# Two SBUF pools for the operands of a cross-attention, and a padded row for its last key block

## The chip, the cores and the metric

The kernel runs on one core of one Trainium2 chip, in one launch. The metric is the device time of that core in microseconds. The host only lays the inputs out; all arithmetic is on the core. Engines are named as the profile names them: PE is TensorE's matmul, PEld its weight load, DVE is VectorE, ACT is ScalarE, POOL is GpSimd, SP issues the DMAs.

## The reference, cut to what matters

The model is two perceiver layers on 8 sequences of 64 tokens with 512 features, and a context of 8 x 1601 rows of 512 features. The change touches the first attention alone:

```python
x = x + L0_xattn(layernorm(x), ctx, Wq, bq, Wkv, bkv, Wo, bo)   # touched
x = x + L0_attn(layernorm(x), ...)      # a state-space scan
x = x + L0_ffn(layernorm(x), ...)       # ternary weights
x = x + L1_xattn(layernorm(x), ctx)     # one head, no projections
x = x + L1_attn(layernorm(x), ...)
x = x + L1_ffn(layernorm(x), ...)

def L0_xattn(query, kv, ...):           # 32 heads, 8 groups of keys, head size 128
    q = (query @ Wq + bq)               # 8 groups x 4 heads
    k, v = split(kv @ Wkv + bkv)        # 1601 keys for each of 8 sequences
    scores = einsum(q, k) / sqrt(128)
    o = einsum(softmax(scores), v)
    return o @ Wo + bo
```

## The kernel before, in words

The first attention is walked by `x_all` as 64 units: 8 sequences, and in each 8 key groups `i`. A unit has the 4 x 64 = 256 queries of one group and goes over the 1601 keys in six blocks (`BLK`): five of 256 keys and a last one of 322, of which 1601 are real keys in all. Both float32 operands of a projection are split in a high and a low part, each of type fp32r, and a product is the sum of three matmuls, (0,0), (0,1) and (1,0). Over the four chunks of 128 features that is 12 matmuls into one PSUM tile. The steps, each with the names that the profile shows:

- `x_ctx` (blocks `cxb`, last block `cxt`): loads a block of the transposed context chunk by chunk into `cst`, and splits it: ACT copies the high part, POOL subtracts for the low part (lines 101 and 102). A block is made once for a sequence and used by all 8 groups.
- `x_k` (line 354, PSUM tile `k_ps`): the keys. The stationary operand is the weight tile `wk`, the moving one is `cxb` with 256 columns or `cxt` with 322. ACT and DVE split the result into `kt` (lines 104, 105).
- `x_v` (line 325, `v_ps`): the values of 128 keys for two groups at once. The stationary operand is 128 columns of `cxb` or `cxt`, the moving one is the weight tile `wv` with 256 columns. ACT copies the result into `v`.
- `x_s` (line 374, `s_ps`): the scores. Stationary `kt`, moving `q`, three matmuls for 128 keys. ACT copies them into `S` (line 377), DVE keeps a running maximum in `mx` (line 381).
- `x_max`, `x_spread`, `x_exp`: of the unit before, the maximum is made one per query, spread over the partitions, subtracted (DVE, line 415) and exponentiated (ACT, line 416); POOL sums into `ss` (lines 418, 426).
- `x_av` (line 438, `o_ps`): stationary `v`, moving `S`, in plain float32.
- `x_o` and `x_wo` (line 495, `w_ps`): normalisation into `ot`, and for each pair of sequences the product with the output weights, stationary `ot`, moving `wo` with 512 columns.

Beside this stream runs side work: `prep` (weights of the later layers are split and stored) and, for each finished pair of sequences, `chain` (all later layers for that pair). The recording order interleaves the two by planned shares, and the engines execute in that order. The last pair's chain stands alone at the end, from about 2400 us on; for it the pools of the first attention are closed and the pool `tp` takes their place.

Tiles come from pools, and a pool's place in SBUF follows from the order in which pools are opened. Before, one pool `xp` holds all tiles of the first attention. The pools `const`, `xw` and `xp` lie from the bottom up; `qp` and later `cp` lie at the top. In the built kernel the tiles stand so (KB from the start of a partition):

| tile | before | after |
|---|---|---|
| `cxb` (5 buffers) | 55.25 to 95.25 | 19.25 to 59.25 |
| `q` | 114.69 to 118.69 | 59.25 to 63.25 |
| `v` (16) | 120.69 to 136.69 | 63.25 to 79.25 |
| `cxt` | 136.69 to 146.75 | 79.25 to 89.75 |
| `ot` | 150.81 to 154.81 | 89.75 to 93.75 |
| `S` (12) | 23.25 to 47.25 | 93.75 to 117.75 |
| `wk` (2) | 47.25 to 55.25 | 117.75 to 125.75 |
| `cst` (3) | 95.25 to 99.09 | 125.75 to 129.69 |
| `kt` (3) | 99.09 to 106.69 | 129.69 to 137.56 |
| `wv` | 106.69 to 114.69 | 137.56 to 145.56 |
| `wo` (3) | 154.81 to 166.81 | 151.62 to 163.62 |

Of the kernel before, what the change touches and what calls it, by code (L numbers as in the profile page):

```python
# [9 lines left out]
FR = mybir.dt.float32r  # L10
# [6 lines left out]
P = 128  # L17
D = 512
NC = 4
T = 64  # L20
LK = 1601
LP = 1602
NKV = 8
G = 4
NT = 13
# [13 lines left out]
VB, SB = 16, 12  # L39
# [36 lines left out]
class Kernel:  # L76
# [214 lines left out]
    def x_ctx(self, b, k):  # L291

        nc = self.nc
        o, w = BLK[k]
        if k == 5:
            t = self.sb("cxt", [P, 2, NC, 322], FR, pool=self.xp, bufs=1)
        else:
            t = self.sb("cxb", [P, 2, NC, 256], FR, pool=self.xp, bufs=5)
        for c in range(NC):
            st = self.sb("cst", [P, 322], pool=self.xp, bufs=3)  # L300
            nc.sync.dma_start(out=st[:, :w], in_=self.i["ctxT"][b, c, :, o : o + w])
            self.split(t[:, 0, c, :], t[:, 1, c, :], st[:, :w], eng=nc.gpsimd)
        self.ctxb[(b, k)] = t
# [6 lines left out]
    def x_v(self, b, j, t):  # L310

        nc = self.nc
        if j not in self.wv_t:
            w = self.sb("wv", [P, 2, NC, 256], FR, pool=self.xp, bufs=1)
            nc.sync.dma_start(out=w.bitcast(FP), in_=self.wv_s[j])
            self.wv_t = {j: w}
        w = self.wv_t[j]
        ps = self.px.tile([P, D], FP, name=self.nm("v_ps"), tag="kv", bufs=KVB)[:, :256]
        blk, o = (5, 256) if t == 12 else (t // 2, (t % 2) * P)
        r = rows_of(t)  # L320
        cx = self.cblk(b, blk)
        k = 0
        for c in range(NC):
            for a, m in ((0, 0), (0, 1), (1, 0)):
                nc.tensor.matmul(ps[:r], lhsT=cx[:, a, c, o : o + r], rhs=w[:, m, c, :], start=k == 0, stop=k == 11)  # L325
                k += 1
        vt = self.sb("v", [P, 256], pool=self.xp, bufs=VB)
        nc.scalar.copy(vt[:r], ps[:r])  # L328
        self.v[(b, j, t)] = vt

# [7 lines left out]
        self.wkt[(b, i)] = w  # L338

    def x_q(self, b, i):  # L340
        q = self.sb("q", [P, 2, 256], FR, pool=self.xp, bufs=2)
        self.nc.sync.dma_start(out=q.bitcast(FP), in_=self.q_s[i][b].rearrange("p l g t -> p l (g t)"))
        self.q[(b, i)] = q

    def x_k(self, b, i, blk, w):

        nc = self.nc
        wd = BLK[blk][1]
        cx = self.cblk(b, blk)
        ps = self.px.tile([P, D], FP, name=self.nm("k_ps"), tag="kv", bufs=KVB)  # L350
        k = 0
        for c in range(NC):
            for a, m in ((0, 0), (0, 1), (1, 0)):
                nc.tensor.matmul(ps[:, :wd], lhsT=w[:, a, c, :], rhs=cx[:, m, c, :], start=k == 0, stop=k == 11)  # L354
                k += 1
        kt = self.sb("kt", [P, 2, 322], FR, pool=self.xp, bufs=3)
        self.split(kt[:, 0, :wd], kt[:, 1, :wd], ps[:, :wd], bias=self.bk[:, i : i + 1])
        return kt

# [80 lines left out]
    def x_o(self, b, i):  # L440

        nc = self.nc
        ps = self.o.pop((b, i))
        self.S.pop((b, i))
        r = self.l.pop((b, i))
        nc.tensor.matmul(ps[:, 1], lhsT=self.ones, rhs=r, start=True, stop=True)
        w = self.sb("rw", [P, 256], pool=self.xp, bufs=1)
        nc.scalar.activation(r, ps[:, 1], AF.Ln)
        nc.scalar.activation(r, r, AF.Exp, scale=-1.0)
        nc.vector.tensor_tensor(w, ps[:, 1], r, ALU.mult)  # L450
        nc.vector.scalar_tensor_tensor(r, w, 2.0, r, ALU.subtract, ALU.mult, reverse0=True)
        oa = w
        nc.vector.tensor_tensor(oa, ps[:, 0], r, ALU.mult)

        odd = b % 2
        oav = oa.rearrange("p (g t) -> p g t", t=T)
        scr = self.ot_s[b // 2][i]
        if b < 2:
            ot = self.sb("ot", [P, 1, G, 2, T], pool=self.xp, bufs=OTB)
            nc.scalar.activation(ot[:, 0, :, odd], oav, AF.Identity, bias=self.bv[:, i : i + 1])  # L460
        else:
            ot = self.sb("ot", [P, 2, G, 2, T], FR, pool=self.xp, bufs=OTB)
            self.split(ot[:, 0, :, odd], ot[:, 1, :, odd], oav, bias=self.bv[:, i : i + 1])
        if odd:
            nc.sync.dma_start(out=ot[:, :, :, 0].bitcast(FP), in_=scr)
            self.ot[(b, i)] = ot
        else:
            nc.sync.dma_start(out=scr, in_=ot[:, :, :, 0].bitcast(FP))
# [507 lines left out]
    def xattn1(self, bs, x, xo):  # L976
# [7 lines left out]
        def scores(k, b):  # L984
            q0 = k * T
            if self.tail:
                s = self.sb("bc", [T, LP])
                S = [s[:, :512], s[:, 512:1024], s[:, 1024:]]
# [252 lines left out]
    def run(self):  # L1241
        nc, tc, ctx = self.nc, self.tc, self.ctx
        nc.scalar.preload_act_table_set("natural_log_exp_and_others")
        self.setup(bufs=BUFS, accb=2, hs=4, tail=False, ahead=1, **TAGS)
        self.pc = ctx.enter_context(tc.tile_pool(name="pc", bufs=2, space=PSUM))
        xctx = ctx.enter_context(ExitStack())
        self.px = xctx.enter_context(tc.tile_pool(name="px", bufs=2, space=PSUM))
        self.consts()
        self.scratch()
        self.xw = ctx.enter_context(tc.tile_pool(name="xw", bufs=2))  # L1250
        self.xp = xctx.enter_context(tc.tile_pool(name="xp", bufs=2))
        qctx = ctx.enter_context(ExitStack())
        self.q_ln(qctx.enter_context(tc.tile_pool(name="qp", bufs=2, side="right")))
        B = self.B
        sizes = GROUPS.get(B) or [1] * B
        groups, k = [], 0
        for m in sizes:
            groups.append(list(range(k, k + m)))
            k += m
        self.place = {b: (k * T, len(g) * T) for g in groups for k, b in enumerate(g)}  # L1260
        side, self.tp = [], None

        def start(gen, now, cost, end):
            env = {k: getattr(self, k) for k in ENV}
            if not self.tail:
                env["nc"] = Side(self, PINNED)
            side.append({"gen": gen, "cost": cost, "got": 0.0, "t0": now, "end": end, "env": env})

        def advance(now):
            base = {k: getattr(self, k, None) for k in ENV}  # L1270
            for c in list(side):
                self.setup(**c["env"])
                goal = c["cost"] * min(1.0, (now - c["t0"]) / max(c["end"] - c["t0"], 1e-9))
                if now >= c["end"]:
                    goal = 1e9
                while c["got"] < goal:
                    try:
                        c["got"] += next(c["gen"])
                    except StopIteration:
                        if PRINT_COST:  # L1280
                            print("side", c["got"])
                        side.remove(c)
                        break
            self.setup(**base)

        gi, now, xdone = 0, 0.0, 0.0
        for cost, fin in self.x_all(list(range(B))):
            xdone += cost
            advance(xdone / X_COST)
            if fin == 0:  # L1290
                qctx.close()
                self.cp = ctx.enter_context(tc.tile_pool(name="cp", bufs=2, side="right"))
                start(self.prep(), xdone / X_COST, PREP_COST, PREP_END)
            if fin is not None and gi < len(groups) and groups[gi][-1] == fin:
                g = groups[gi]
                now = xdone / X_COST
                last = gi == len(groups) - 1
                if last:
                    self.pinning = False
                    xctx.close()  # L1300
                    self.pc = ctx.enter_context(tc.tile_pool(name="pt", bufs=3, space=PSUM))
                    self.cp = self.tp = ctx.enter_context(tc.tile_pool(name="tp", bufs=2))
                    self.setup(bufs=BUFS_TAIL, accb=6, hs=8, tail=True, ahead=2, **TAGS_TAIL)
                start(self.chain(gi, g), now, CHAIN_COST, now + SPAN[gi])
                if last:
                    side.insert(0, side.pop())
                gi += 1
        while side:
            now += 0.01
            advance(now)  # L1310
# [10 lines left out]
OTB = 1  # L1321
# [35 lines left out]
def _layout(inp):  # L1357
# [7 lines left out]
    r["ctxN"] = cx  # L1365
    ct = np.zeros((B, D, LP), f)
    ct[:, :, :LK] = np.transpose(cx, (0, 2, 1))
# [68 lines left out]
```

## Time and profile before

| | us |
|---|---|
| median of 3 runs | 2748.9 |
| lowest and highest | 2741.76, 2750.92 |
| the profiled execution | 2747.45 |
| its span, first to last instruction | 2745.6 |
| PE busy in it | 2584.6 |
| stretch from 60 to 2400 us: PE busy | 2281.36 of 2340.00 |
| stretch from 2400 us to the end: PE busy | 260.00 of 345.60 |

The profile is of one execution, whose time lies between the lowest and the highest of the runs. Matmul records overlap: each reaches from the issue to the modelled end of its last column, so a record is longer than the distance to the next one. The distance from start to start tells how fast PE goes through a group.

### The profile page before, as it was taken

How to read it: one execution, taken by the hardware profiler on the slowest of the kernel's cores; microseconds unless marked ns; L12 is line 12 of the kernel's file. 1: busy time of each engine (PE TensorE's matmuls, PEld its weight loads, DVE VectorE, ACT ScalarE, POOL GpSimd, SP SyncE). 2: the span in 40 equal slices, each digit the busy share in tenths (PEclk: the TensorE clock that was granted, in tenths of full speed). 3: DMA queues.
4: the chain of work that ended last, by engine and by line, in shares of the span. 5: the costliest groups of instructions: out<-in, count | busy, mean ns of one | idle time of the engine just before them, and what ended most of it. 6: DMA issues, size and time to landing. Idle time of an engine off the chain costs nothing.

```text
span 2745.6 us, 47783 instructions
## 1 busy us (share of the span) xinstructions
PE 2584.6 (94%) x17840; PEld 2303.7 (84%) x17840; DVE 1756.7 (64%) x2988; ACT 1378.4 (50%) x3318; POOL 1163.1 (42%) x1175
## 2 busy tenths in 40 slices
PE   7999999999999899999999989999999999976778
PEld 6999999889889899978988988988897998954545
DVE  4544345577777886545587787454668787549645
ACT  4444555444556554544456555444556555435433
POOL 3212444474579653421367344421348435215220
PEclk9999999999999999999999999999999999978889
DMA  9544446664666234664325534665333543465676
GB/s 305 151 144 152 131 155 221 204 205 156 212 208 212 71 116 164 215 192 155 114 78 156 156 106 131 199 203 165 125 101 97 168 153 126 146 221 197 219 253 218
DMA packets 312167, 460.03 MB, mean 168 GB/s; under 512 B 81272, under 2 KB 188792, under 8 KB 307456
## 3 DMA queue, kind: packets, MB, share of 16 engines
q1 hardware_dynamic: 311936, 456.99, 51.6%
q8 instruction: 140, 2.29, 0.3%
q14 instruction: 91, 0.75, 0.1%
HBM read 384.42 MB, written 72.48 MB: 166 GB/s over the span
## 4 chain that ended last, share of the span: by engine, by line
PE 60%; DVE 15%; DMA 9%; POOL 7%; issue 5%; ACT 4%; SPq 1%; POOLq 0%; DVEq 0%; ACTq 0%
PE v_ps L325 14%; PE k_ps L354 13%; PE o_ps L438 8%; PE s_ps L374 7%; DVE a L62 4%; PE w_ps L495 3%; POOL a L62 3%; PE acc L270 2%; POOL ss L426 2%; PE acc L1000 2%; PE acc L1053 2%; PE acc L740 2%; DMA cst<-in_ctxT_dram 2%; PE acc L743 1%; PE acc L785 1%
## 5 line engine op out<-in xcount | busy, mean ns | idle before, releaser
L354 PE MATMUL k_ps<-cxb,wk 128*128 128x256 f32 x3840 | 560.9, 291 | 21.8 <-ACT cxb L101 9.6
L354 PEld LDWEIGHTS k_ps<-cxb,wk 128*128 128x128 f32 x3840 | 504.9, 191 | 55.8 <-issue 15.1
L325 PE MATMUL v_ps<-wv,cxb 128*128 128x256 f32 x3840 | 521.5, 283 | 7.4 <-DVE mx L381 3.3
L325 PEld LDWEIGHTS v_ps<-wv,cxb 128*128 128x128 f32 x3840 | 479.2, 189 | 28.2 <-issue 13.9
L374 PE MATMUL s_ps<-q,kt 128*128 128x256 f32 (+1 forms) x2496 | 414.9, 299 | 13.3 <-DVE kt L105 4.9
L438 PE MATMUL o_ps<-S,v 128*128 128x256 f32 (+1 forms) x1664 | 409.2, 380 | 1.7 <-ACT S L416 1.6
L374 PEld LDWEIGHTS s_ps<-q,kt 128*128 128x128 f32 (+1 forms) x2496 | 339.7, 185 | 38.0 <-DVE kt L105 7.2
L381 DVE TENSOR_TENSOR mx<-s_ps,mx 128x512 f32<-128x512 f32 x256 | 175.3, 685 | 306.5 <-ACT S L377 306.3
L426 POOL TENSOR_TENSOR ss<-ss,S 128x512 f32<-128x512 f32 x256 | 355.0, 1387 | 16.2 <-ACT S L416 1.5
L377 ACT COPY S<-s_ps 128x512 f32<-128x512 f32 (+1 forms) x448 | 241.5, 551 | 211.8 <-PE s_ps L374 210.7
L438 PEld LDWEIGHTS o_ps<-S,v 128*128 128x128 f32 (+1 forms) x1664 | 296.4, 190 | 33.9 <-ACT S L416 2.5
L418 POOL TENSOR_TENSOR ss<-S,S 128x512 f32<-128x512 f32 x64 | 84.2, 1316 | 566.2 <-ACT S L416 566.0
L104 ACT ACTIVATE kt<-k_ps,c_bk 128x256 fp32r<-128x256 f32 (+1 forms) x384 | 184.7, 481 | 220.1 <-PE k_ps L354 216.1
L105 DVE SCALAR_TENSOR_TENSOR kt<-k_ps,c_bk,kt 128x256 fp32r<-128x256 f32 (+1 forms) x384 | 187.7, 489 | 144.0 <-ACT kt L104 143.2
L415 DVE TENSOR_TENSOR S<-S,m_ps 128x512 f32<-128x512 f32 (+1 forms) x448 | 257.6, 641 | 28.6 <-PE m_ps L401 27.6
L416 ACT ACTIVATE S<-S 128x512 f32<-128x512 f32 (+1 forms) x448 | 247.2, 599 | 42.5 <-DVE S L415 41.9
L328 ACT COPY v<-v_ps 128x256 f32<-128x256 f32 (+1 forms) x416 | 152.3, 367 | 219.6 <-PE v_ps L325 217.9
L62 ACT ACTIVATE a<-lv,c_A_log 128x128 f32<-128x128 f32 x384 | 122.7, 392 | 126.6 <-DVE lv L62 120.3
L62 POOL TENSOR_TENSOR a<-bc,lv 128x512 f32<-128x512 f32 x96 | 128.2, 1336 | 127.7 <-DVE a L62 112.4
L102 POOL TENSOR_TENSOR cxb<-cst,cxb 128x256 fp32r<-128x256 f32 x160 | 126.3, 804 | 120.9 <-ACT cxb L101 118.0
L62 DVE TENSOR_TENSOR_SCAN a<-a,a 128x512 f32<-128x512 f32 x96 | 145.1, 1512 | 48.3 <-POOL a L62 47.9
L325 PE MATMUL v_ps<-wv,cxt 128*128 128x256 f32 (+1 forms) x1152 | 161.8, 286 | 2.2 <-DVE kt L105 2.2
(348 smaller groups left out, 3972.0 us busy)
## 6 DMA issues: line engine op xcount, KB each, us to landing
wo<-d_wo SPq DMA_DIRECT2D x96, 512.0 KB, 4.9
wk<-d_wk SPq DMA_DIRECT2D x63, 512.0 KB, 3.4
wv<-d_wv SPq DMA_DIRECT2D x31, 1024.0 KB, 7.0
cst<-in_ctxT_dram SPq DMA_DIRECT2D x160, 128.0 KB, 3.1
b<-in_ctxN_dram SPq DMA_DIRECT2D x36, 512.0 KB, 4.2
d_q<-q_t SPq DMA_DIRECT2D x32, 512.0 KB, 4.3
q<-d_q SPq DMA_DIRECT2D x64, 256.0 KB, 3.6
d_wo<-b SPq DMA_DIRECT2D x32, 512.0 KB, 2.9
```

Source lines behind the costliest of these rows:

```text
L62: return lambda *a, **k: self.tc.keep_in_program_order(f(*a, **k))
L104: nc.scalar.activation(hi, src, AF.Identity, bias=bias)
L105: eng.scalar_tensor_tensor(lo, src, bias, hi.bitcast(FP), ALU.add, ALU.subtract)
L325: nc.tensor.matmul(ps[:r], lhsT=cx[:, a, c, o : o + r], rhs=w[:, m, c, :], start=k == 0, stop=k == 11)
L354: nc.tensor.matmul(ps[:, :wd], lhsT=w[:, a, c, :], rhs=cx[:, m, c, :], start=k == 0, stop=k == 11)
L374: nc.tensor.matmul(sp[:r, gi, :], lhsT=kt[:, a, u * P : u * P + r], rhs=q[:, m, :], start=k == 0, stop=k == 2)
L377: nc.scalar.copy(s[:r, :n], sp[:r, :n])
L381: nc.vector.tensor_tensor(mx, sp, S[0] if len(S) == 1 else mx, ALU.max)
L415: nc.vector.tensor_tensor(sv, sv, ps[:r, 1:2].to_broadcast([r, w, 256]), ALU.add)
L416: nc.scalar.activation(sv, sv, AF.Exp, scale=ISC)
L426: nc.gpsimd.tensor_tensor(ss, ss, S[n], ALU.add)
L438: nc.tensor.matmul(ps[:, 0], lhsT=self.v[(b, j, t)][:r, hc : hc + P], rhs=S[t // 2][:r, t % 2], start=t == 0, stop=t == NT - 1)
```

## The change

One pool becomes two. The new pool `xl` is opened before `xp` and takes `cxb`, `cxt`, `v`, `q` and `ot`; `xp` keeps `S`, `wk`, `wv`, `kt`, `wo`, `cst` and the small tiles, and so begins at 93.75 KB. The pool `xw` moves to the top end, which lets everything else at both ends slide down by 4 KB. Of the five products each now has one operand in `xl` and the other in `xp`. The tiles for the last block get rows of 336 elements (1344 bytes) in place of 322 (1288 bytes); the matmuls, copies and loads still run over 322.

```diff
+KW = 336
...
         if k == 5:
-            t = self.sb("cxt", [P, 2, NC, 322], FR, pool=self.xp, bufs=1)
+            t = self.sb("cxt", [P, 2, NC, KW], FR, pool=self.xl, bufs=1)[:, :, :, :w]
         else:
-            t = self.sb("cxb", [P, 2, NC, 256], FR, pool=self.xp, bufs=5)
+            t = self.sb("cxb", [P, 2, NC, 256], FR, pool=self.xl, bufs=5)
         for c in range(NC):
-            st = self.sb("cst", [P, 322], pool=self.xp, bufs=3)
+            st = self.sb("cst", [P, KW], pool=self.xp, bufs=3)
...
-        vt = self.sb("v", [P, 256], pool=self.xp, bufs=VB)
+        vt = self.sb("v", [P, 256], pool=self.xl, bufs=VB)
...
-        q = self.sb("q", [P, 2, 256], FR, pool=self.xp, bufs=2)
+        q = self.sb("q", [P, 2, 256], FR, pool=self.xl, bufs=2)
...
-        kt = self.sb("kt", [P, 2, 322], FR, pool=self.xp, bufs=3)
+        kt = self.sb("kt", [P, 2, KW], FR, pool=self.xp, bufs=3)
...
-            ot = self.sb("ot", [P, 1, G, 2, T], pool=self.xp, bufs=OTB)
+            ot = self.sb("ot", [P, 1, G, 2, T], pool=self.xl, bufs=OTB)
...
-            ot = self.sb("ot", [P, 2, G, 2, T], FR, pool=self.xp, bufs=OTB)
+            ot = self.sb("ot", [P, 2, G, 2, T], FR, pool=self.xl, bufs=OTB)
...
-        self.xw = ctx.enter_context(tc.tile_pool(name="xw", bufs=2))
+        self.xw = ctx.enter_context(tc.tile_pool(name="xw", bufs=2, side="right"))
+
+        self.xl = xctx.enter_context(tc.tile_pool(name="xl", bufs=2))
         self.xp = xctx.enter_context(tc.tile_pool(name="xp", bufs=2))
```

The buffer counts are the same. In the built kernels every engine has the same instructions in the same order, SP's DMA issues included, and each waits for the same semaphores; what differs is addresses and the stride between rows of the last block.

## The prediction

> **What bounds the kernel now.** I read the page's busy lines first, then busy time by stretch, then the sources of the three projection and score lines, then a piece of PE's timeline.
>
> ```profile
> span 2745.6 us, 47783 instructions
> PE 2584.6 (94%) x17840; PEld 2303.7 (84%) x17840; DVE 1756.7 (64%) x2988; ACT 1378.4 (50%) x3318; POOL 1163.1 (42%) x1175
> ```
> ```profile
> 300.00:600.00 300.00, 297.72 (x2138) 277.65 (x2137) 164.21 (x312) 152.50 (x346) 152.47 (x153) 1.00 0.58 184
> 600.00:900.00 300.00, 280.82 (x2031) 263.90 (x2030) 228.10 (x361) 167.37 (x407) 197.30 (x194) 0.98 0.60 198
> ```
>
> The columns after the length of a stretch are busy PE, PEld, DVE, ACT and POOL, then the granted clock. PE is busy 297.72 of 300 us in the first stretch shown, and 2281.36 of 2340 (97.5%) from 60 to 2400 us. The exception is 600 to 900 us, where PE idles 19 us and POOL and DVE are busiest. So until 2400 us the time is PE's instruction count times PE's pace, and a change that leaves the instructions alone must act on the pace. The last 345.6 us belong to another pool and keep their layout but for a shift of 4 KB.
>
> The sources, limited to 60 to 2400 us (duration minimum/median/maximum in ns):
>
> ```profile
> L354 PE MATMUL k_ps<-cxb,wk x3786: 274/283/682, 59.8 to 2387.3; 128*128 128x256 f32 x200
> L325 PE MATMUL v_ps<-wv,cxb x3816: 275/277/682, 61.4 to 2374.9; 128*128 128x256 f32 x191
> L325 PE MATMUL v_ps<-wv,cxt x1152: 274/281/683, 94.0 to 2393.8; 128*128 128x256 f32 x128, 128*65 128x256 f32 x64
> L374 PE MATMUL s_ps<-q,kt x2478: 274/281/775, 64.3 to 2398.4; 128*128 128x256 f32 x191
> ```
>
> These are four groups of one shape, 256 moving columns on 128 stationary ones, and they do not take the same time: 277 ns where the moving tile is `wv` and the stationary one `cxb`, 281 to 283 ns elsewhere. PE's timeline shows the same in the distance between starts:
>
> ```profile
> 72.05 1.59 PE L354 MATMUL k_ps<-cxb,wk 128*128 128x256 f32 x12
> 73.48 2.90 PE L325 MATMUL v_ps<-wv,cxb 128*128 128x256 f32 x24
> 76.22 1.21 PE L374 MATMUL s_ps<-q,kt 128*128 128x256 f32 x9
> ```
>
> From 72.05 to 73.48 are 12 key matmuls, 119 ns each; from 73.48 to 76.22 are 24 value matmuls, 114 ns each. Nothing waits between. Over the whole trace, start to start within a group, distances of 150 ns and more (a wait) left out, the means are: keys on `cxb` 118.9 ns, values on `cxb` 115.5, values on `cxt` 118.4, scores 117.9. 59% of the values on `cxb` follow within 115 ns, but 1% of the keys, 9% of the values on `cxt` and 10% of the scores.
>
> Against the table of places: `wk` and `cxb` both lie below 96 KB, `kt` and `q` both above, `wv` and `cxt` both above; only `wv` and `cxb` lie on different sides. The one pair that is split is the one that is fast. It is no load from outside: split by whether ACT, DVE or POOL was running or DMA packets were in flight, each group's mean moves by under 1.2 ns.
>
> **The change, part by part.** It removes, adds and moves no instruction, DMA or wait, so no queue gains an entry and nothing new is queued behind a wait. The sum has these terms, each the count times the difference to the split pair's 115.5 ns:
>
> - Keys on `cxb`: 3840 x (118.9 - 115.5) = 13.1 us. After, `cxb` is below and `wk` above.
> - Scores: 2496 x (117.9 - 115.5) = 6.0 us. `q` goes below, `kt` stays above. Padding `kt` is within this: scores whose stationary rows begin on 64 bytes run at 117.4, the others at 118.0.
> - Values on `cxt`: 1152 x (118.4 - 115.5) = 3.3 us. `cxt` goes below; its rows become aligned.
> - Keys on `cxt`, 322 columns, 768 of them: this pair was split before (`cxt` above, `wk` below), so only the padding acts. Rows that happen to begin on 64 bytes go at 147.3 ns, the others at 148.4: 768 x 1 = under 1 us, taken as 0.5. The upper bound is the split pair's rate by column, 113.4 / 256 x 322 = 142.6, which would be 4 us.
> - Values on `cxb`: split before and after; 0. Probabilities times values (line 438) are plain float32, were split before and stay so but for `S`'s first two buffers: 0. Output product (line 495): 288 fp32r matmuls at 229.7 ns whose commonest distance is 227: 0 to 0.8, taken as 0.
> - Other engines: tiles that move are read or written by POOL, ACT and DVE. POOL's split (line 102) takes 738 ns in the median with both inputs below 96 KB and 741 with `cst` above, ACT's copy 406 and 407. Taken as 0 either way; should it cost 3 ns on the 192 splits, that is 0.6 us and PE's work covers it. If that cover were gone it would still be 0.6.
>
> Sum: 22.9 us of PE pace. Not all reaches the end. In the stretch 600 to 900 us, 13% of the 2340, PE waits for POOL and DVE already, and a faster PE only waits longer there. What becomes late next is the same list that PE waits for now, `mx` and `kt` from DVE, some 60 us in all. I keep 87%: 20 us. From the profiled 2747.45 that gives 2727.5. The profiled run stands 1.45 below the median of 2748.9, so I say 2728.
>
> Bounds of the unknown price. Above: if every such pair went at the fast level of 113.4 ns (the 59%), keys save 3840 x 5.5 = 21.1, scores 2496 x 4.5 = 11.2, values on `cxt` 1152 x 5 = 5.8, keys on `cxt` 3.9, and the values on `cxb` themselves 3840 x 2.1 = 8.1: 50 us, 44 after the 87%, so 2704. Below: nothing, or the second rival's loss. I take the means, since a split pair has shown these and not the ideal.
>
> The Trainium skill speaks against the change. "SBUF — State Buffer", section "Who interferes with whom", gives PE two independent read ports, one for the moving operand and one for weight loads, and says that PE never waits on anyone; by that rule the places of the two operands cannot matter and the sum is 0. The rows above do not fit it: two groups of one shape differ by 6 ns in the median with no other engine's part in it. The page names no boundary inside a partition.
>
> **Rivals.**
>
> 1. The side of 96 KB is not the cause; keys are slow for another reason, such as their fixed pair of weights or low address bits. Against it: values on `cxt` use the same `wv` and the same loop and lose the fast pace. For it: with 512 moving columns pairs on one side often reach the best pace seen (the output product, both above, 227 ns, just twice 113.4), and in the tail a pair on two sides (line 1200) runs at 228 to 232. Then only alignment is left, 1 to 3 us: 2746, no change that can be told.
>
> 2. Slower: the fast pace of the values hangs on where exactly `wv` lies, and moving it from 106.69 to 137.56 KB loses it. The offset within 1 KB goes from 704 to 576 bytes. Then 3840 values go at the keys' 118.9: +13.1 us, and keys and scores gain nothing: 2747.45 + 13.1 = 2760.5, or 2762 against the median. It decides as soon as the values' loss exceeds the other groups' gain, that is from a mean of 115.5 + 22.9 / 3840 x 1000 = 121.5 ns if all others gain, or any rise at all if none does. For it: the levels inside the values group (113, 118, 121) show that side alone does not fix the pace. Against it: all five `cxb` buffers, at five distances from `wv`, give means of 116 to 123 ns (short waits included), with none slow throughout.
>
> 3. PE gets faster and the time does not follow, because DVE and POOL end last. In 300 to 600 us DVE is busy 55% and POOL 51%, so only 600 to 900 speaks for it; the gain would be halved, 2738. It lies inside the forecast's range.
>
> **How the numbers follow.** A measurement of this kernel can tell about 0.3%, 8 us, from no change. The forecast (with the third rival) has 0.63, its own range 2704 to 2740; no effect 0.17; slower by the second rival 0.20. Each case lies on its own side of the 8 us, so faster by over 0.3% is 0.63, within 0.3% 0.17, slower 0.20. To hold 8 in 10 the range must reach past no change up to the second rival's figure: 2704 to 2762.
>
> **What would show it.** In the changed kernel's source views the key matmuls on `cxb` fall from a median of 283 to 277 to 279 ns, scores and values on `cxt` from 281 to 277 or 278, values on `cxb` stay at 277, keys on `cxt` stay within 2 ns of 310; PE busy falls by about 20 us from 2584.6 and the idle time in 600 to 900 us grows. The step about sides is wrong if keys stay at 283, the step about `wv` if values on `cxb` rise above 279, and the 87% if PE's busy time falls and the span does not. A lower granted clock before 2400 us than now (0.99) would make all of it unreadable.

## The result: 0.3% slower, by the values' matmuls

The changed kernel takes 2759.3 us in the median of 13 runs, the kernel before 2749.4 in 13: a ratio of 1.0032, 95% interval 1.0023 to 1.0042. The forecast was 2728, and faster. The second rival came out, in its direction and in the group of matmuls that it named.

The page of the changed kernel, span and busy time by engine:

```profile
span 2759.7 us, 47783 instructions
PE 2597.8 (94%) x17840; PEld 2314.4 (84%) x17840; DVE 1760.0 (64%) x2988; ACT 1381.9 (50%) x3318; POOL 1165.6 (42%) x1175
```

PE has the same 17840 matmuls and is busy 13.2 us longer; the span grew by 14.1 (this one execution lies farther from the one of before than the medians do, which differ by 9.9). DVE, ACT and POOL are within 4 us of what they were. So the loss is in PE, and the sources say in which group of matmuls (60 to 2400 us, duration minimum/median/maximum in ns; the lines moved by two with the diff):

```profile
L356 PE MATMUL k_ps<-cxb,wk x3773: 274/283/682, 59.7 to 2399.9; 128*128 128x256 f32 x199
L327 PE MATMUL v_ps<-wv,cxb x3816: 275/279/681, 61.0 to 2388.7; 128*128 128x256 f32 x191
L327 PE MATMUL v_ps<-wv,cxt x1128: 274/280/681, 93.8 to 2397.2; 128*128 128x256 f32 x126, 128*65 128x256 f32 x62
L376 PE MATMUL s_ps<-q,kt x2457: 274/281/775, 63.9 to 2397.9; 128*128 128x256 f32 x189
```

Keys stayed at 283 although their operands are now on two sides of 96 KB. Scores stayed at 281. Values on `cxb`, which were to stay at 277, went to 279. The timeline has the same place in the program as before:

```profile
71.68 1.59 PE L356 MATMUL k_ps<-cxb,wk 128*128 128x256 f32 x12
73.10 2.99 PE L327 MATMUL v_ps<-wv,cxb 128*128 128x256 f32 x24
75.93 1.23 PE L376 MATMUL s_ps<-q,kt 128*128 128x256 f32 x9
```

From 73.10 to 75.93 are 24 value matmuls, 118 ns each, where they took 114; the 12 keys before them still take 118 to 119. Over the whole trace the mean from start to start (distances of 150 ns and more left out, as in the prediction) is 117.6 ns for the values, from 115.5, and the share within 115 ns fell from 59% to 8%. 3840 x 2.06 ns = 7.9 us.

Since both kernels have the same PE instructions in the same order, the two traces can be subtracted interval by interval. From the first matmul to the last the changed kernel takes 13.8 us more. The distances that are under 150 ns in both traces account for 6.5 of them: 6.9 more in the values on `cxb`, and near nothing in all other groups together. The other 7.2 us lie in longer distances, which hold wide matmuls and waits, and differ by several us between any two executions: 5.9 us between the traces of the kernel before and of e1 below, whose times are the same by their ratio.

### The profile page after: what moved, and what is told of

Read it like the earlier page. It is cut to its first block, busy times and chain, and to the rows that moved or that the text cites. A ratio compares the mean times of both kernels' runs of the same rounds, so it can differ in the third digit from the quotient of the medians.

```text
span 2759.7 us, 47783 instructions
## 1 busy us (share of the span) xinstructions
PE 2597.8 (94%) x17840; PEld 2314.4 (84%) x17840; DVE 1760.0 (64%) x2988; ACT 1381.9 (50%) x3318; POOL 1165.6 (42%) x1175
## 4 chain that ended last, share of the span: by engine, by line
PE 61%; DVE 15%; DMA 8%; POOL 7%; issue 4%; ACT 4%; SPq 1%; POOLq 0%; DVEq 0%; ACTq 0%
PE v_ps L327 14%; PE k_ps L356 13%; PE o_ps L440 8%; PE s_ps L376 7%; DVE a L64 5%; PE w_ps L497 3%; POOL a L64 2%; PE acc L272 2%; DMA cst<-in_ctxT_dram 2%; PE acc L1002 2%; PE acc L742 2%; PE acc L787 2%; POOL ss L428 2%; PE acc L1055 2%; PE acc L745 2%
## 5 line engine op out<-in xcount | busy, mean ns | idle before, releaser
L104 POOL TENSOR_TENSOR cxb<-cst,cxb 128x256 fp32r<-128x256 f32 x160 | 125.4, 799 | 122.7 <-ACT cxb L103 116.6
```

## The experiments

After the result the question was what makes a pair fast, if not the side. In the kernel before, the start of the stationary operand lies 64 bytes after that of the moving one for the values (`cxb` at 256 within 1 KB, `wv` at 704, taken modulo 256 bytes), and 0 bytes for the keys (`wk` and `cxb` both at 256 modulo 1 KB). In the changed kernel it is 192 and 0. These two groups keep their distance from matmul to matmul, since all their steps are multiples of 512 bytes. Theory F: this fine distance sets the pace (F256 in later expectations: the distance modulo 256 bytes does). Theory P: the large place in SBUF does. Theory S: the sides of 96 KB do, and something spoils it.

Tiles were moved inside longer tiles, so that no edit adds, removes or moves an instruction. For `wv` (cut; the same replacement stands at the place where `wv` is first filled):

```diff
-            w = self.sb("wv", [P, 2, NC, 256], FR, pool=self.xp, bufs=1)
+            w = self.wvt()
...
+    def wvt(self):
+
+        t = self.sb("wv", [P, 2176], FR, pool=self.xp, bufs=1)
+        return t[:, 32 : 2080].rearrange("p (a c w) -> p a c w", a=2, c=NC)
```

The number of elements left free ahead of the data, here 32 (128 bytes), is called the front below.

**e1, the changed kernel with `wv` 128 bytes further** (the diff above; all after it is shifted by 512 bytes).

> The changed kernel with the weight tile wv moved up by 128 bytes and nothing else by a fine step: it still lies above 137 KB, cxb below 60 KB, but its start within 1 KB is 704 bytes again, as before the change, in place of 576. Theory F (the pace hangs on the fine offset between the two operands' starts, modulo a few hundred bytes, not on the side of 96 KB): values on cxb go back from a mean of 117.6 ns from start to start to 115.5, their median record from 279 to 277 ns, and the time falls by 3840 x 2.1 = 8 us to about 2751. Theory P (the pace hangs on the large place: which part of SBUF wv and cxb lie in): values stay at 117.6 and the time at 2759.

Measured: 2750.04 us, ratio to the kernel before 0.9999 (0.9985 to 1.0013). Values 115.5 ns, keys 119.3. The values' source, and the timeline at the place shown above:

```profile
L327 PE MATMUL v_ps<-wv,cxb x3816: 276/276/683, 61.0 to 2381.6; 128*128 128x256 f32 x191
```
```profile
71.59 1.59 PE L361 MATMUL k_ps<-cxb,wk 128*128 128x256 f32 x12
73.02 2.90 PE L327 MATMUL v_ps<-wv,cxb 128*128 128x256 f32 x24
75.76 1.23 PE L381 MATMUL s_ps<-q,kt 128*128 128x256 f32 x9
```

24 values take 2.74 us again, 114 ns each. 128 bytes undo the values' whole loss, and the loss in time with it: the interval lies apart from the changed kernel's. `wv` and `cxb` still lie where the changed kernel puts them, so theory P is out.

**e2, the kernel before with `wv` 896 bytes further** (front of 224 elements in a tile of 2304).

> The kernel before with wv moved up by 896 bytes inside a tile 1 KB longer: its start within 1 KB is 576 bytes, as in the changed kernel, and it stays near 107 KB; all that comes after it is shifted by exactly 1 KB. Theory F: values on cxb slow down from 115.5 to 117.6 ns and the time rises by 8 us to about 2757. Theory P: values stay at 115.5 and the time at 2749.

Measured: values 117.5 ns, the median record 279; ratio 1.0004 (0.9989 to 1.0019), 2753.45 us.

```profile
L325 PE MATMUL v_ps<-wv,cxb x3816: 275/279/681, 61.0 to 2381.9; 128*128 128x256 f32 x191
```

The pace is just that of the changed kernel, with everything near its old place. The time did not follow as expected: 2757 was forecast, and the interval, which includes no change, allows at most 5 us of the 7.5 that the pace is worth. That part was missed.

**m1, a map of distances** (`cxb` buffers of 2064 elements, `wk` buffers of 1104, `wv` with a front of 16 in a tile of 2064, so that each buffer of `cxb` and `wk` stands at another fine offset).

> A map from one profile: the kernel before with the five cxb buffers 64 bytes further apart than their size and the second wk buffer 320 bytes further off, so that the ten pairs of key matmuls have all eight distances of their starts modulo 512 bytes (in steps of 64), and the values five of them (wv keeps its offset). Theory F: the pace changes from pair to pair by up to 5 ns, the same distance gives keys and values the same pace, distance 0 gives 119 and distance 64 gives 115.5 ns. Theory P: all ten key pairs run at 118.9 ns and all five value pairs at 115.5. The time is not what is asked; it should lie within 15 us of 2749.

**m2, the same in half steps** (2056 and 1064 elements).

> The map in steps of 32 bytes: cxb buffers 32 bytes and wk buffers 160 bytes further apart than their size, so key pairs stand at 0, 32, 64, ... 224 bytes modulo 256, and values at 160, 192, 224, 0 and 32. Theory F256 as it stands: 64 stays the only fast distance, with 32 and 96 between their neighbours (0: 119, 64: 116, 128: 119). If the grain is coarser, 32 or 96 is as fast as 64. Theory P: all pairs alike.

Mean ns from start to start by the distance, in bytes modulo 256, of the stationary start after the moving one (where several pairs of buffers share a distance, the mean of them):

| distance | keys m1 | keys m2 | values m1 | values m2 |
|---|---|---|---|---|
| 0 | 119.2 | 119.1 | 119.3 | 119.2 |
| 32 | | 118.3 | | 118.3 |
| 64 | 115.8 | 115.7 | 115.3 | |
| 96 | | 117.8 | | |
| 128 | 119.3 | 118.5 | 118.0 | |
| 160 | | 119.5 | | 119.4 |
| 192 | 117.7 | 117.6 | 116.8 | 116.4 |
| 224 | | 117.0 | | 117.3 |

Keys and values, with their operands' roles exchanged, follow one curve to within 1.3 ns, and 64 is the fastest. The table goes by 256 because in m1, where the ten key pairs stand at eight distances modulo 512, pairs that differ by 256 agree within 0.4 ns. That is not the whole rule. In m2 the two key pairs at 64 and 320 modulo 512 take 115.2 and 116.3 ns. For the values, 192 and 448 modulo 512 take 117.7 and 116.0 ns in m1, and 448 takes 116.4 in m2, while the changed kernel, e2 and e5, all at 192, take 117.5 to 117.7. So the distance modulo 256 tells the pace to about 1.5 ns, and something finer is left open. The times of single runs were 2755.68 and 2757.53 us.

**e3, the keys moved to 64** in the kernel before (`wk` in buffers of 1152 elements, front 16).

> The kernel before with both wk buffers moved up by 64 bytes against cxb (modulo 512 bytes), all other tiles shifted by exactly 1 KB: the stationary operand of the keys then starts 64 bytes after the moving one, which is the distance that the fast values have. Theory F in its simplest form (the distance alone decides): keys on cxb go from 118.9 to about 115.5 ns, the time falls by 3840 x 3.4 = 13 us, of which 87% arrive: about 2738. If the offset matters in another way: keys change, but not to 115.5. Theory P: keys stay at 118.9, time at 2749.

Measured: keys 116.5 ns, values 116.2 at an unchanged distance, ratio 0.9988 (0.9972 to 1.0005), 2749.52 us. The keys gained 3840 x 2.5 = 9.6 us of pace, the values lost 2.8, and the interval for the time allows a gain of up to 8 us or none. The simple form, 115.5 for the keys and 13 us, was too good.

**e4, the two pools without the padding** (the edit in full).

```diff
-KW = 336
+KW = 322
```

> The changed kernel without the padding (rows of 322 as before), so the two pools alone. The shorter tiles move what follows: wk now starts 64 bytes after cxb modulo 256 bytes (0 before and in the changed kernel), and cxb starts 0 bytes after wv (64 before, 192 in the changed kernel). Theory F256 (the pace of a group hangs on the distance of the stationary from the moving start modulo 256 bytes: 64 fast, 192 middling, 0 and 128 slow): keys on cxb 118.9 to about 116.4 ns, values on cxb 115.5 to about 119.3; net 3840 x (3.8 - 2.5) = +5 us, time about 2755. Rival S (sides of 96 KB matter and the padding alone spoils it): keys and values both at 115.5, time about 2730. Rival P (the large place): values at 117.6 as in the changed kernel, keys at 119, time about 2759.

Measured: keys 115.5 ns, values 119.6; ratio 1.0018 (1.0005 to 1.0030), 2752.34 us. The sources and a piece of the timeline:

```profile
L356 PE MATMUL k_ps<-cxb,wk x3780: 275/278/774, 71.1 to 2388.0; 128*128 128x256 f32 x199
L327 PE MATMUL v_ps<-wv,cxb x3816: 274/283/682, 60.4 to 2375.6; 128*128 128x256 f32 x191
```
```profile
77.13 1.53 PE L356 MATMUL k_ps<-cxb,wk 128*128 128x256 f32 x12
78.50 3.04 PE L327 MATMUL v_ps<-wv,cxb 128*128 128x256 f32 x24
81.38 0.40 PE L376 MATMUL s_ps<-q,kt 128*128 128x256 f32 x2
```

The groups have changed places: keys in 1.37 us for 12 (114 ns), values in 2.88 for 24 (120). The operands of both products lie on two sides of 96 KB here, one is fast and the other slow. Theory S is out, and the fine distance told beforehand which of the two would be fast: the values to 0.3 ns, the keys, said to be 116.4, to 0.9.

**e5, the padding alone**, in one pool (`cxt`, `cst` and `kt` with rows of 336 in the kernel before).

> The kernel before with the padded rows alone, all in one pool. The longer rows move wv by 384 bytes, so cxb starts 192 bytes after wv modulo 256, as in the changed kernel; keys keep distance 0. Theory F256: values on cxb 117.5 ns, keys 118.9, time 4 to 8 us above the kernel before. Rivals S and P: values stay at 115.5, time as before, or 1 us less for the aligned rows.

Measured: values 117.7, keys 119.1; ratio 1.0023 (1.0012 to 1.0034), 2756.08 us. The time rose by 6.3 us (3.3 to 9.3), within what was expected. The longer rows move `wv`, which is allocated after them, and with it the values' distance from 64 to 192. Padding that was to align rows slows the kernel here by what it shifts.

```profile
L326 PE MATMUL v_ps<-wv,cxb x3816: 275/279/775, 61.7 to 2387.9; 128*128 128x256 f32 x191
```

**e6, a higher dose**: the kernel before with `wv` 64 bytes further (front 16, tile of 2304), values at distance 0.

> A dose test: the kernel before with wv moved so that cxb starts 0 bytes after it modulo 256; nothing else changes by a fine step. Theory F256: values on cxb at 119.3 ns, 3.8 more than before, 3840 x 3.8 = 14.6 us of PE pace, of which the changed kernel's ratio of pace to time (7.9 us for values, 10 in all) says that nearly all arrive: 2760 to 2765. If a good part of the pace is lost in waits elsewhere: under 2758. Rivals S and P: 2749.

Measured: values 119.6 ns, their median record as long as the keys' in the kernel before; ratio 1.0032 (1.0021 to 1.0043), 2756.66 us. 3840 x 4.1 = 15.7 us of pace became 2748.36 x 0.0032 = 8.8 us (5.8 to 11.8) of time: a little over half. The expected 2760 was missed, and the other case, under 2758, came; that the missing part is lost in waits was not shown.

```profile
L325 PE MATMUL v_ps<-wv,cxb x3816: 274/283/682, 61.5 to 2384.4; 128*128 128x256 f32 x191
```

**e7 and e9, all three groups at 64** in one pool (`wk` in buffers of 1088 elements, front 16; `cst` of 336; `kt` as below). e9 is e7 once more, beside e8.

```diff
-        kt = self.sb("kt", [P, 2, 322], FR, pool=self.xp, bufs=3)
+        kt = self.sb("kt", [P, 704], FR, pool=self.xp, bufs=3)[:, 16 : 16 + 2 * wd].rearrange("p (a w) -> p a w", a=2)
```

> A version that should beat both: one pool as before, wk shifted by 64 bytes, kt with rows of the block's own width and buffers of 2816 bytes, so that keys, values and scores (of the five blocks of 256) all have the stationary start 64 bytes after the moving one modulo 256 bytes. Theory F256: keys 116.3, values 115.5, scores about 116; PE pace falls by 3840 x 2.6 + 1900 x 1.9 = 13.6 us; time 2736 to 2743, the upper end if waits take back half, as they did with the keys alone. Rivals S and P: 2749.

> e7 once more, beside e8 on the same chip, so that the two can be compared: keys 116.5, values 116.0, scores 117.0 ns, ratio to the kernel before 0.998.

Measured: keys 116.6 and 116.5 ns, values 116.0 in both, scores 117.0 in both; ratios 0.9981 (0.9968 to 0.9994) and 0.9980 (0.9967 to 0.9994), 2744.97 and 2746.93 us. Two profiles of one kernel thus agree within 0.1 ns in the pace of all three groups, which says how far the paces above can be trusted. The medians lie 2 and 4 us above the forecast 2736 to 2743. Both intervals lie below 1 and below the changed kernel's, by little.

**e8, the same distances in the two pools** (rows of 322 but for `cst`, `kt` as in e7, `wv` with a front of 48).

> Does the side of 96 KB add anything at the good distance? The two pools with rows of 322, kt in buffers of 2816 bytes, and wv shifted, so that keys, values and scores (of the five blocks of 256) all have the stationary start 64 bytes after the moving one modulo 256 bytes, as in e7, but with the two operands of each product below and above. Theory F256 with no part for the sides: keys, values and scores as in e7 (116.5, 116.0, 117.0), time as e7, about 2744. If the split sides add: keys and values at 115.5 or less, time 2736 to 2740.

Measured: keys 116.1, values 116.0, scores 117.5; ratio 0.9968 (0.9956 to 0.9981), 2744.2 us against 2751.84 of the kernel before on that chip. Its sources:

```profile
L361 PE MATMUL k_ps<-cxb,wk x3789: 275/281/684, 59.8 to 2386.7; 128*128 128x256 f32 x200
L327 PE MATMUL v_ps<-wv,cxb x3816: 275/280/708, 61.8 to 2374.3; 128*128 128x256 f32 x191
```

Paces as in e7 to within 0.5 ns. The interval overlaps those of e7 and e9, so no gain from the sides is shown. Its profiled execution, 2751.86 us, is the slowest of its six, so its span isn't read. It has the lowest ratio of all versions tried: 0.3% below the kernel before, and by the two ratios 0.6% below the changed one, beside which it was not run.

## Why the prediction was wrong, step by step

**What bounds the kernel.** Right in direction. PE's pace moves the time: shifts of 64 to 128 bytes, with no instruction added, removed or moved, changed it by up to 0.3% either way (e6, e8). But it is not one to one, as the paragraph on the 87% tells.

**The reading that failed** is the sentence "The one pair that is split is the one that is fast". It was true of the rows and it was no cause. In the kernel before, each of the four groups of 256 columns has one layout, and for the two with constant steps the side of 96 KB and the fine distance told the same story: values split and at 64, keys on one side and at 0. The trace of before could not part the two; the table of places held both, and the prediction used it only for the large place. The runs show that the fine distance sets the two paces and the side does not (e1, e4). From the failed reading came the terms of the sum:

- Keys on `cxb`, 13.1 us: measured 118.9 to 119.2, a loss of 1 us. Distance 0 before and after.
- Scores, 6.0 us: 117.9 to 118.0, nothing.
- Values on `cxt`, 3.3 us: 118.4 to 118.0, a gain of 0.4 us.
- Keys on `cxt`, 0.5 us: 148.2 to 148.6, a loss of 0.2. Rows that begin on 64 bytes brought nothing here; the fine distance of this pair differs from row to row and changed with the padding, so the two can't be told apart.
- Values on `cxb`, "split before and after; 0": the term that mattered. Being split was kept and the pace was lost: 115.5 to 117.6 ns, a loss of 3840 x 2.06 = 7.9 us where the sum has 0.
- Output product, 0: 229.7 to 232.1, 288 x 2.4 = 0.7 us. Its tiles went from distance 0 to 128; no run tests this group by itself.
- Other engines, 0: their busy times grew by 2.5 to 3.5 us each; no effect of that on the time was separated.

**The second rival** had the mechanism ("the fast pace of the values hangs on where exactly `wv` lies", with 704 going to 576) and the sign. Its size was off: it took the keys' 118.9 as the price of the lost place, and distance 192 costs 117.6. The argument raised against it, that five `cxb` buffers at five distances were all fast, said nothing: those distances are all equal modulo 256. It deserved more weight: with the "low address bits" of the first rival it named a variable in which keys and values of the kernel before differ apart from their side. The first rival had that right for the keys, and missed that the same bits would slow the values.

**The skill's rule** was weighed as speaking against any effect: "SBUF — State Buffer", "Who interferes with whom", gives PE two independent read ports and says that it never waits on anyone. Read as "places cannot matter", it makes the change worth 0, which is nearer to 2759 than 2728. That reading went too far: the rule is about ports and other engines, and the runs show a pace that hangs on the two operands' own addresses, some 4 ns of 119 by 64 bytes. The measurement decides.

**The 87%** was a guess at what arrives, and the runs give no single share. In the changed kernel nearly all arrived: about 9.6 us by the groups above and 8.8 (6.3 to 11.5) in time. In e6 it was a little over half. For e7 the groups' sum, 3840 x 2.4 + 2496 x 0.9 - 3840 x 0.5 = 9.5 us, became 2748.36 x 0.0019 = 5.2 (1.6 to 8.8), and in e2 the 7.5 us of the values became 1.1 (at most 5.2).

The prediction's list of waits was read too large: from 60 to 2400 us PE's waits for `mx` and `kt` come to 29.9 us of 56.5 in all, not "some 60". Its idle time is spread wider than the one stretch it named, too: 19.2 us in 600 to 900, but 12.4 in 1500 to 1800. Where the missing part goes was not settled. In e6's trace PE idles 14.2 us in 600 to 900, against 19.2 before and 18.2 in e1, which fits a slower PE that waits less there; but that is one execution each, and waits change by several us from one to the next, as much as what is looked for. A slip beside this: 2748.9 less 20 is 2728.9, so the sum says 2729 rather than 2728.

**What stays open.** Why the pace changes with the distance, and why 64 is good, was not tried. What is shown holds for fp32r matmuls of 256 columns on 128 stationary ones. Within a group at 64 the distance from start to start still jumps between 113 and 118 ns. Values at an unchanged 64 went from 115.5 to 116.2 when the keys moved in e3, and stood at 116.0 in e7 and e8, where the keys are at 64 as well; that a group's neighbour matters is a guess from this. And e2 and e5, with the same pace for the values, differ in time by 5 us by their ratios, though the intervals overlap.

## What to carry to other kernels

When two groups of one shape run at two paces, list everything in which their operands differ, the low address bits included, before a cause is named; a cause that fits one fast and three slow groups is not yet told from another that fits them as well. A change of a tile's length or of a pool's order moves all that is allocated after it, so compare the fine offsets of the operands on the bounding engine in both builds, and fix them on purpose where they matter. A rule found in one trace is cheaply tested by a map: give each buffer another offset and read all distances from one profile.

## What the runs showed of the hardware that was not expected

- The pace of back-to-back fp32r matmuls of 256 columns depends on the distance between the starts of the stationary and the moving operand, for the most part modulo 256 bytes: 115.2 to 116.6 ns at 64, 116.0 to 117.9 at 192, 117.0 to 117.3 at 224, 118.0 to 119.6 at 0, 128 and 160, over all pairs and runs here. 32 bytes to either side of 64 it is already about 118.
- The side of 96 KB showed no part in it beyond half a ns: keys at 0 take 118.9 ns on one side and 119.2 split; at 64 they take 115.7 to 116.6 on one side and 115.5 to 116.1 split. The values were not tried with both operands on one side.
- Plain float32 did not care: probabilities times values (each matmul stands as two records in the trace) take 216.3 ns from the start of one record to the next at distance 192 (before) and 0 (after), and 216.2 at 64 (e5).
